# Raw statistics held behind the table's last part, all third parts copied by VectorE, and the bias's parts spread by one product, in a graph layer's kernel

## The chip, the cores and the metric

The kernel runs on one core of a Trainium2 chip. The metric is the device time of one execution in microseconds (us); the time before is the median of three runs. The engines are called PE (TensorE, matrix products), ACT (ScalarE), DVE (VectorE), POOL (GpSimd) and SP (SyncE, which here only issues DMAs). PEld is TensorE's weight load. "L504" is line 504 of the kernel before.

## What is computed

A graph layer with 12,500 nodes of 128 features, 200,000 edges and 4 edge types. Edges are sorted by their target node; sources and types are random, and the targets crowd toward low node numbers. Cut to what matters:

```python
h = jnp.maximum(_layernorm(x, axis=-1), 0.0)          # x: 12500 x 128, fp32
xs = h[src]                                            # 200000 rows
msgs = 0
for i in range(4):                                     # W: 4 x 128 x 128, b: 4 x 128
    msgs = msgs + jnp.where((edge_type == i)[:, None], xs @ W[i] + b[i], 0.0)
out = x + jax.ops.segment_sum(msgs, dst, num_segments=12500)
```

## The kernel before

The kernel sums source rows per target node and type first and multiplies by W afterwards. Edges come in chunks of 128. A one-hot matrix of a chunk (edge by target and type) turns the sum into a TensorE product. The lowest target nodes have so many edges that they go another way: edges are counted per node, type and source, and the counts are multiplied with the whole of h. It has three stages, which overlap.

**The table and the slots (0 to about 119 us).** h is written to DRAM as a table (`htab`), each fp32 number as three bf16 parts whose sum is that number. The nodes are cut into 33 spans of up to three rows for each of the 128 partitions. For each span:

- `load_span` loads x by SP (L190 to L192) into one of 11 buffers (`hm`).
- `look` gives five steps as functions: the statistics of each row (`bn_stats`, DVE, L440), their sums (DVE, L444 to L449), the root (ACT, L452), the scales (DVE, L455 and L456) and the normalisation with relu (ACT, L461).
- `first_part` normalises and copies h to the first bf16 part (ACT, L487), and PE puts h minus that part into PSUM (L490 and L491).
- `second_part` copies that difference to the second part (ACT, L496), and PE subtracts it too (L497).
- `third_part` copies what is left to the third part: for odd spans by ACT (L502), for even ones by DVE (L504). Then SP writes the span's three parts to `htab` (L506). The difference lies in one of four PSUM banks in turn (two named `ps`, one `py`, one `pa`), and the three parts in one of five buffers `h3`.

The parts of neighbouring spans are taken in turn: first part of span u, second part of u − 1, third part of u − 2. Between them the code also issues steps of `ring_rows`, a generator that prepares small things. Among these are the bias's three bf16 parts, as `b12` (12 rows: part c of type t in row 4c + t) and as `b128` (128 rows: part c of type t in row 32t + c, all other rows zero). It zeroes `b128` (DVE, L1180), then copies the 12 rows one by one with 12 DMAs of SP (L1196, 256 bytes each). `b128` is first used by the main loop's weighting (`weigh`, L605), `b12` by the slots and the raw groups.

The slots are the work list of the dense part. `make_slots` finds for each of the lowest nodes where its edges lie: DVE one-hots (L816) times edge data on PE (L825, L854, L857), unpacking and comparing on DVE (L837 to L842, L866 to L871, L883 to L897, L913 to L918), a product that counts edges by type (PE, L903), its copy with a running sum (ACT, L904), the bias's share of these nodes (PE, L925) and its copy (ACT, L933). One-hots, products and copies of the 512-column pieces are pipelined by generators; their PSUM tiles are the four `pt` banks.

**The raw groups (to about 157 us).** The first 48 chunks don't wait for the table. Their rows of x are gathered by GpSimd (`gather_raw`, L528) while the table is made. Then `add_up_raw` treats them in three groups of 16: statistics (L440, tile `str`), sums, root, scales, normalisation in place (L461, tile `hx`), one-hots (DVE, L620), and fp32 products (PE, L635, L641, L646, L648) with copies by ACT (L636, L643). The normalisations of raw rows are also marks that the first gathers of the main loop from `htab` (POOL, L544) are tied to.

**The main loop (to 1649 us).** All other chunks in groups of 16: gathers from `htab` (L544), one-hots (L561), products (L578), copies (L581), weighting (L596 to L605), and adding into a ring of node sums (L666). The dense part runs beside it: one-hots (L957, L965), counts (L983, L989) and the products of counts with h (L1033), for which SP loads `htab` back in order (L1029).

The program is written in one order, and a scheduler that works from the program's dependences orders each engine's instructions before the run. An engine then works strictly in its order. The function `held_by` adds a dependence by hand, which both orders two instructions and makes the second wait for the first.

Of the kernel before, what the change touches and what calls it, by code (L numbers as in the profile page):

```python
# [35 lines left out]
F32 = mybir.dt.float32  # L36
BF16 = mybir.dt.bfloat16
# [11 lines left out]
P = 128  # L49
# [25 lines left out]
def kernel(  # L75
# [10 lines left out]
    nc = tc.nc  # L86
    N, D = x.shape
    E = src.shape[0]
    NT, _, DO = w.shape
# [7 lines left out]
    N3 = 3 * NT  # L97
# [10 lines left out]
    q = E0 / E  # L108
# [37 lines left out]
    for i, n in enumerate(sizes_of):  # L146
# [4 lines left out]
        of = alone[3 * many_at : 3 * (many_at + n1)]  # L151
# [269 lines left out]
    CG = P // NT  # L421
# [10 lines left out]
    def look(xt, n, tag, wide):  # L432

        sums2 = aheads.tile([P, wide, 2], F32, name="mv" + tag)
        var = aheads.tile([P, wide], F32, name="var" + tag)
        rstd = aheads.tile([P, wide], F32, name="rstd" + tag)
        nmr = aheads.tile([P, wide], F32, name="nmr" + tag)
        st = aheads.tile([P, wide, 2, 3], F32, name="st" + tag)
        looks = [
            lambda k=k: nc.vector.bn_stats(st[:, k].rearrange("p h s -> p (h s)"), xt(k)).ins for k in range(n)  # L440
        ]

        def spread():
            nc.vector.tensor_tensor(sums2[:, :n], st[:, :n, 0, 1:], st[:, :n, 1, 1:], ALU.add)  # L444
            nc.vector.tensor_tensor(var[:, :n], st[:, :n, 0, 1], st[:, :n, 1, 1], ALU.subtract)
            nc.vector.scalar_tensor_tensor(
                var[:, :n], var[:, :n], 0.25 * D, var[:, :n], op0=ALU.mult, op1=ALU.mult
            )
            nc.vector.tensor_tensor(var[:, :n], var[:, :n], sums2[:, :n, 1], ALU.add)  # L449

        def root():
            nc.scalar.activation(rstd[:, :n], var[:, :n], AF.Sqrt, bias=eps, scale=1.0 / D)  # L452

        def scales():
            nc.vector.reciprocal(rstd[:, :n], rstd[:, :n])  # L455
            nc.vector.scalar_tensor_tensor(  # L456
                nmr[:, :n], sums2[:, :n, 0], -0.5, rstd[:, :n], op0=ALU.mult, op1=ALU.mult
            )

        def normalize(k, h):  # L460
            return nc.scalar.activation(  # L461
                h, xt(k), AF.Relu, bias=nmr[:, k : k + 1], scale=rstd[:, k : k + 1]
            ).ins

        return looks, spread, root, scales, normalize
# [11 lines left out]

    banks = [(s_ps, "ps"), (s_ps, "ps"), (y_ps, "py"), (a_ps, "pa")]
    splits = {}

    def first_part(u, one):
        n = spans[u][1] - spans[u][0]
# [15 lines left out]

    def third_part(u):
        ps, h3, n = splits.pop(u)  # L500
        if u % 2:
            nc.scalar.copy(h3[:, :n, 2, :], ps)  # L502
        else:
            nc.vector.tensor_copy(h3[:, :n, 2, :], ps)  # L504
        j0, j1 = spans[u]
        nc.sync.dma_start(  # L506
            htab.rearrange("(p j) f -> p j f", j=NW)[:, j0:j1, :], h3[:, :n].rearrange("p j c d -> p j (c d)")
        )
# [8 lines left out]
    def held_by(one, by, reason):  # L517
        tc.add_manual_dep(
            one.ins,
            by.name,  # L520
            mybir.DependencyInfo(mybir.DependencyClass.Sync, mybir.DependencyReason.DATA),
            reason=reason,
        )
# [86 lines left out]
    def add_up_raw(t0, g, rows, marked):  # L610
        win = window_of(C0 + t0)
        K = NT * win
        row = lambda k: rows(k)
        looks, spread, root, scales, normalize = look(row, g, "r", G)
        for l in looks:
            l()
        spread()
        root()
        oh = rawp.tile([P, G, KR], F32, name="ohf", bufs=2)[:, :, :K]
        nc.vector.tensor_tensor(  # L620
            oh,
            iota_f[:, :K].unsqueeze(1).to_broadcast([P, g, K]),
            keyf[:, t0 : t0 + g].unsqueeze(2).to_broadcast([P, g, K]),
            ALU.is_equal,
        )
        yield True
        scales()
        done = [normalize(k, row(k)) for k in range(g)]
        marked.extend(done[4::5])
        yield True  # L630
        sb = spool.tile([P, G * KM], F32, name="sb")[:, : G * K].rearrange("p (g t n) -> p g t n", g=G, t=NT)
        for i0 in range(0, g, SG):
            ps = s_ps.tile([P, 512], F32, name="ps")[:, : SG * K].rearrange("p (i n) -> p i n", i=SG)
            for i in range(i0, i0 + SG):
                nc.tensor.matmul(ps[:, i - i0, :], rows(i), oh[:, i, :], start=True, stop=True)  # L635
            nc.scalar.copy(sb[:, i0 : i0 + SG].rearrange("p g t n -> p g (t n)"), ps)  # L636
            yield True
        ohv = oh.rearrange("p g (t n) -> p g t n", t=NT)
        pc = s_ps.tile([P, 512], F32, name="ps")[:N3, : G * win].rearrange("p (g n) -> p g n", g=G)
        for t in range(NT):  # L640
            nc.tensor.matmul(pc, pick_f[:, t, :], ohv[:, :, t, :], start=(t == 0), stop=(t == NT - 1))  # L641
        cnt = spool.tile([N3, G * WIN], BF16, name="cnt")[:, : G * win].rearrange("p (g n) -> p g n", g=G)
        nc.scalar.copy(cnt, pc)  # L643
        yield True
        py = raw_py[:, t0 * win : (t0 + g) * win].rearrange("p (g n) -> p g n", g=G)
        nc.tensor.matmul(py, b12, cnt, start=True, stop=False)  # L646
        for t in range(NT):
            nc.tensor.matmul(py, wsb[:, t, :], sb[:, :, t, :], start=False, stop=(t == NT - 1))  # L648
        yield True
# [521 lines left out]
    def ring_rows():  # L1171
        nc.vector.tensor_single_scalar(over, heads, RING.bit_length() - 1, op=ALU.arith_shift_right)
        nc.vector.scalar_tensor_tensor(heads, over, -float(RING), heads, op0=ALU.mult, op1=ALU.add)
        nc.vector.tensor_scalar(heads, heads, 0.0, float(RING - 1), ALU.max, ALU.min)
        nc.sync.dma_start(heads_d, heads)
        nc.sync.dma_start(brow, heads_d.rearrange("(o q) c -> o (q c)", o=1))
        yield True
        part12 = prep.tile([N3, 3], F32, name="part12")
        nc.vector.tensor_reduce(part12, ident[:N3, :N3].rearrange("p (c t) -> p c t", c=3), AX.X, ALU.add)
        nc.vector.memset(b128, 0.0)  # L1180
        bs = prep.tile([N3, DO], F32, name="bs")
        for c in range(3):
            bh = prep.tile([N3, DO], BF16, name="bh")
            nc.vector.tensor_copy(bh, bf)
            if c == 0:
                nc.vector.tensor_scalar(bs, bh, part12[:, 0:1], None, ALU.mult)
            else:
                nc.vector.scalar_tensor_tensor(bs, bh, part12[:, c : c + 1], bs, op0=ALU.mult, op1=ALU.add)
            if c < 2:
                nc.vector.tensor_sub(bf, bf, bh)  # L1190
            yield True
        nc.vector.tensor_copy(b12, bs)
        for t in range(NT):
            for c in range(3):
                k = c * NT + t
                nc.sync.dma_start(b128[t * CG + c : t * CG + c + 1, :], b12[k : k + 1, :])  # L1196
        yield True

    group_of = []
# [20 lines left out]
    for gi, us in enumerate(group_of):  # L1220
        here, at_here = ahead, at
        more_looks = []
        if gi + 1 < len(group_of):
            for u in group_of[gi + 1]:
                while len(queue) <= u:
                    queue.append(load_span(len(queue)))
            ahead, at = look_at(group_of[gi + 1])
            more_looks = list(ahead[0])
        each = -(-len(more_looks) // max(1, len(us) - 1))
        for i, u in enumerate(us):  # L1230
            while len(queue) < min(NU, u + 14):
                queue.append(load_span(len(queue)))
            first_part(u, lambda k, h: here[4](at_here[u, k], h))
            if u:
                second_part(u - 1)
            if u > 1:
                third_part(u - 2)
            last = None
            for l in more_looks[:each]:
                last = l()  # L1240
            del more_looks[:each]
            while last is not None and len(raws) < min(NRAW, 3 + (u + 1) * NRAW // (NU - 4)):
                raws.append(gather_raw(len(raws), last))
            if gi + 1 < len(group_of):
                if i == max(0, len(us) - 2):
                    ahead[1]()
                    ahead[2]()
                if i == len(us) - 1:
                    ahead[3]()
            if u >= 3:  # L1250
                next(small, None)
# [270 lines left out]
```

## Time and profile before

| | us |
|---|---|
| median of three runs | 1648.86 (1646.37 to 1652.16) |
| profiled execution, its own time | 1651.06 |
| profiled execution, span of the trace | 1649.2 |
| PE busy in the span | 1457.4 (88%) |
| DVE busy | 1041.5 (63%) |
| POOL busy | 1011.6 (61%) |
| ACT busy | 458.7 (28%) |

The span runs from the first to the last instruction; the execution's own time has 1.86 us more around it. A group of instructions is shown as: line, engine, operation, out<-in, (partitions x elements, type), count | busy us, mean ns of one | idle time of that engine just before them, and what ended it. A row of a timeline is: start, length, engine, line, operation, out<-in, count, and in brackets the idle time before it and what released it; "issue" means that the engine waited for nothing that the profile shows. Records of neighbouring instructions can overlap by some tenths of a microsecond. A queue row (SPq) is the time in which SP issues a DMA, not the transfer.

### The profile page before, as it was taken

The numbers are of one execution on the slowest core, as the hardware profiler recorded it, in microseconds if no ns is written. First come the engines' busy times: TensorE is split into PE (matmuls) and PEld (weight loads), VectorE is DVE, ScalarE is ACT, GpSimd is POOL, SyncE is SP. The second block draws the span as 40 slices with busy tenths as digits, with TensorE's granted clock in tenths as the row PEclk, the third lists the DMA queues.
The fourth block names the chain that finished last, engine by engine and source line by source line (L and its number), as shares of the span: only waits on it lengthen the run. The fifth ranks groups of instructions, "written<-read, shape, count | busy, mean of one in ns | idle before, by whom it ended". The sixth has DMA issues, their size and how long they took to land.

```text
span 1649.2 us, 33169 instructions
## 1 busy us (share of the span) xinstructions
PE 1457.4 (88%) x11293; PEld 958.5 (58%) x11293; DVE 1041.5 (63%) x5387; ACT 458.7 (28%) x1121; POOL 1011.6 (61%) x1062
## 2 busy tenths in 40 slices
PE   5678789999899999999999999999999999998975
PEld 2236476666566566666666666656565656565654
DVE  8792977666585766657576666657564756574333
ACT  6494222222222222222222222222222222222011
POOL 7435566666666666666666666666666566666562
PEclk9785799999999999999999999999999999999997
DMA  7452377766667766666666667666666566666652
GB/s 221 129 212 75 107 220 220 217 197 213 200 206 211 217 194 212 197 208 208 207 202 201 200 209 220 181 210 203 180 219 198 175 194 211 184 189 193 210 169 70
DMA packets 138411, 317.02 MB, mean 192 GB/s; under 512 B 25880, under 2 KB 78666, under 8 KB 138235
## 3 DMA queue, kind: packets, MB, share of 16 engines
q1 hardware_dynamic: 89323, 214.61, 41.7%
q0 software_dynamic: 48912, 100.24, 20.8%
q8 instruction: 89, 1.46, 0.4%
q14 instruction: 87, 0.71, 0.1%
HBM read 298.71 MB, written 16.04 MB: 191 GB/s over the span
## 4 chain that ended last, share of the span: by engine, by line
PE 81%; issue 8%; DVE 8%; ACT 2%; DMA 1%; DVEq 0%; SPq 0%; POOL 0%; ACTq 0%
PE pa L1033 47%; PE pt L983 12%; PE py L605 7%; PE ps L578 7%; DVE o L957 1%; PE pt L1047 1%; PE ps L635 1%; PE py L596 1%; PE pt L691 1%; DVE oh L561 1%; DVE o L965 1%; DVE ring L666 1%; PE pt L857 1%; DVE stt L440 1%; PE pt L854 0%
## 5 line engine op out<-in xcount | busy, mean ns | idle before, releaser
L544 POOL DMA_INDIRECT hm<-htab,srcT x987 | 954.7, 967 | 575.6 <-issue 226.0
L1033 PE MATMUL pa<-counts,hs 128*128 128x324 fp8e4 (+1 forms) x5586 | 1000.5, 304 | 50.2 <-issue 47.1
L1033 PEld LDWEIGHTS <-hs 128*128 128x128 bf16 x5586 | 519.0, 96 | 325.1 <-issue 84.7
L957 DVE TENSOR_SCALAR o<-iota_n,hkT 128x392 bf16<-128x392 f16 x1211 | 401.2, 331 | 75.4 <-PE pt L983 30.6
L983 PE MATMUL pt<-o,o 128*128 128x396 bf16 x1211 | 378.4, 336 | 37.0 <-DVE o L965 20.0
L989 ACT CAST counts<-pt 128x396 int32<-128x396 f32 x506 | 242.1, 493 | 500.5 <-PE pt L983 172.1
L561 DVE TENSOR_SCALAR oh<-iota_b,keyT 128x56 bf16<-128x56 bf16 (+8 forms) x987 | 167.7, 261 | 265.6 <-PE ps L578 94.6
L581 ACT COPY sb<-ps 128x224 f32<-128x224 f32 (+8 forms) x247 | 98.4, 399 | 480.3 <-PE pt L983 165.0
L578 PE MATMUL ps<-oh,hm 128*128 128x56 bf16 (+8 forms) x2961 | 189.1, 198 | 38.0 <-issue 35.3
L578 PEld LDWEIGHTS <-hm 128*128 128x128 bf16 x2961 | 163.0, 99 | 96.5 <-issue 49.1
L666 DVE TENSOR_TENSOR ring<-ring,py 128x14 f32 (+7 forms) x960 | 167.7, 175 | 65.0 <-PE pa L1033 13.0
L965 DVE TENSOR_SCALAR o<-iota,loT 128x128 bf16<-128x128 bf16 x660 | 178.4, 270 | 0.0
L983 PEld LDWEIGHTS <-o 128*128 128x128 bf16 x1211 | 114.8, 97 | 96.2 <-DVE o L965 27.4
L965 DVE TENSOR_SCALAR o<-iota,loT,byT 128x128 bf16<-128x128 bf16 x461 | 155.4, 337 | 0.0
L605 PE MATMUL py<-sb,wsb 128*128 128x224 f32 (+7 forms) x480 | 129.5, 412 | 1.3 <-issue 1.0
L605 PEld LDWEIGHTS py<-sb,wsb 128*128 128x128 f32 x480 | 88.2, 196 | 27.6 <-issue 5.6
L997 DVE COPY bi<-counts 128x27 int32<-128x27 int32 (+1 forms) x19 | 4.2, 220 | 113.3 <-issue 64.7
L528 POOL DMA_INDIRECT hx<-in_x_dram,srcT x48 | 51.3, 1069 | 35.9 <-DVE stt L440 22.4
L600 ACT CAST cnt<-py 128x224 bf16<-128x224 f32 (+7 forms) x60 | 23.7, 396 | 93.3 <-PE ps L578 29.9
L461 ACT ACTIVATE h<-hm,nmrt,rstdt 128x128 f32<-128x128 f32 x98 | 43.0, 493 | 1.0 <-DVE mvt L444 0.5
L1047 PE MATMUL pt<-sd,wsb 128*128 128x81 f32 (+1 forms) x152 | 25.8, 325 | 4.6 <-issue 4.6
L490 PE MATMUL ps<-h,ident 128*128 128x384 f32 (+1 forms) x34 | 16.3, 563 | 12.7 <-issue 11.6
(235 smaller groups left out, 666.6 us busy)
## 6 DMA issues: line engine op xcount, KB each, us to landing
hs<-htab SPq DMA_DIRECT2D x304, 576.0 KB
hm<-htab,srcT POOLq DMA_INDIRECT x987
htab<-h SPq DMA_DIRECT2D x32, 288.0 KB
xo<-in_x_dram SPq DMA_DIRECT2D x24, 256.0 KB
out_dram<-xo SPq DMA_DIRECT2D x24, 256.0 KB
hs<-htab SPq DMA_DIRECT2D x19, 192.0 KB
hm<-in_x_dram SPq DMA_DIRECT2D x18, 192.0 KB
hm<-in_x_dram SPq DMA_DIRECT2D x14, 168.0 KB
```

The source lines that it names most:

```text
L528: one = nc.gpsimd.indirect_dma_start(out=hm[:, i * D : (i + 1) * D], out_offset=None, in_=x, in_offset=bass.IndirectOffsetOnAxis(ap=srcf[: ...
L544: one = nc.gpsimd.indirect_dma_start(out=hm[:, (i - h0) * D3 : (i - h0 + 1) * D3], out_offset=None, in_=htab, in_offset=bass.IndirectOffse ...
L561: nc.vector.tensor_scalar(oh[:, i, :], iota_b[:, :K], keyf[:, at : at + 1], None, ALU.is_equal)
L578: nc.tensor.matmul(ps[:, i - i0, :], rows(i, c), oh[:, i, :], start=(c == 0), stop=(c == 2))
L581: nc.scalar.copy(sb[:, i0:i1].rearrange("p g t n -> p g (t n)"), ps[:, : i1 - i0, :])
L605: nc.tensor.matmul(py[:, :g, :], wsb[:, t, :], sb[:, :g, t, :], start=False, stop=(t == NT - 1))
L666: nc.vector.tensor_tensor(to, to, of(i), ALU.add)
L957: one = nc.vector.tensor_scalar(o2[:, k, :NB], iota_n, hkT[:, s : s + 1], None, ALU.is_equal)
L965: one = nc.vector.tensor_scalar(o1[:, k], iota_1, loT[:, s : s + 1], by, ALU.is_equal, ALU.mult)
L983: one = nc.tensor.matmul(pb, o1, o2, start=first, stop=last)
L989: nc.scalar.copy(counts[:, :, i * NT : (i + 1) * NT], pb.rearrange("p (b t) -> p b t", t=NT))
L1033: nc.tensor.matmul(pa[:, : 3 * nu * NT].rearrange("p (m v) -> p m v", m=3), hs[:, j - j0, c * D : (c + 1) * D], of, start=(j == 0 and c == 0),
```

## The change

Four edits:

1. `third_part` always copies by VectorE, and keeps each copy instruction in the list `thirds`.
2. `look`'s statistics functions return the instruction's handle (callers take `.ins` where they need it), and in `add_up_raw` the first statistics instruction of the second and third group (t0 is 16 or 32) is held by the last entry of `thirds`, which is the copy of the table's last third part.
3. `b128` is no longer zeroed and filled by 12 DMAs. A 12 x 128 bf16 matrix `spread12` with a one at (4c + t, 32t + c) is made from the identity (GpSimd memset, one DVE copy); PE multiplies it with `b12` into a `pt` bank, and DVE copies the bank to `b128`. The product's entries are single bf16 values, so `b128` is the same.
4. `look_at`'s loop takes `.ins` of what `look` returns, without any other effect.

```diff
--- before.py
+++ after.py
@@ -437,7 +437,7 @@
         nmr = aheads.tile([P, wide], F32, name="nmr" + tag)
         st = aheads.tile([P, wide, 2, 3], F32, name="st" + tag)
         looks = [
-            lambda k=k: nc.vector.bn_stats(st[:, k].rearrange("p h s -> p (h s)"), xt(k)).ins for k in range(n)
+            lambda k=k: nc.vector.bn_stats(st[:, k].rearrange("p h s -> p (h s)"), xt(k)) for k in range(n)
         ]
 
         def spread():
@@ -477,6 +477,7 @@
 
     banks = [(s_ps, "ps"), (s_ps, "ps"), (y_ps, "py"), (a_ps, "pa")]
     splits = {}
+    thirds = []
 
     def first_part(u, one):
         n = spans[u][1] - spans[u][0]
@@ -498,10 +499,7 @@
 
     def third_part(u):
         ps, h3, n = splits.pop(u)
-        if u % 2:
-            nc.scalar.copy(h3[:, :n, 2, :], ps)
-        else:
-            nc.vector.tensor_copy(h3[:, :n, 2, :], ps)
+        thirds.append(nc.vector.tensor_copy(h3[:, :n, 2, :], ps).ins)
         j0, j1 = spans[u]
         nc.sync.dma_start(
             htab.rearrange("(p j) f -> p j f", j=NW)[:, j0:j1, :], h3[:, :n].rearrange("p j c d -> p j (c d)")
@@ -612,8 +610,10 @@
         K = NT * win
         row = lambda k: rows(k)
         looks, spread, root, scales, normalize = look(row, g, "r", G)
-        for l in looks:
-            l()
+        for k, l in enumerate(looks):
+            one = l()
+            if t0 and not k:
+                held_by(one, thirds[-1], "rows of x are looked at behind the table")
         spread()
         root()
         oh = rawp.tile([P, G, KR], F32, name="ohf", bufs=2)[:, :, :K]
@@ -1177,7 +1177,6 @@
         yield True
         part12 = prep.tile([N3, 3], F32, name="part12")
         nc.vector.tensor_reduce(part12, ident[:N3, :N3].rearrange("p (c t) -> p c t", c=3), AX.X, ALU.add)
-        nc.vector.memset(b128, 0.0)
         bs = prep.tile([N3, DO], F32, name="bs")
         for c in range(3):
             bh = prep.tile([N3, DO], BF16, name="bh")
@@ -1190,10 +1189,14 @@
                 nc.vector.tensor_sub(bf, bf, bh)
             yield True
         nc.vector.tensor_copy(b12, bs)
-        for t in range(NT):
-            for c in range(3):
-                k = c * NT + t
-                nc.sync.dma_start(b128[t * CG + c : t * CG + c + 1, :], b12[k : k + 1, :])
+        spread12 = prep.tile([N3, P], BF16, name="spread12", bufs=1)
+        nc.gpsimd.memset(spread12, 0.0)
+        nc.vector.tensor_copy(
+            spread12.rearrange("k (t q) -> k t q", q=CG)[:, :, :3], ident[:N3, :N3].rearrange("k (c t) -> k t c", t=NT)
+        )
+        pb = x_ps.tile([P, DO], F32, name="pt")
+        nc.tensor.matmul(pb, spread12, b12, start=True, stop=True)
+        nc.vector.tensor_copy(b128, pb)
         yield True
 
     group_of = []
@@ -1237,7 +1240,7 @@
                 third_part(u - 2)
             last = None
             for l in more_looks[:each]:
-                last = l()
+                last = l().ins
             del more_looks[:each]
             while last is not None and len(raws) < min(NRAW, 3 + (u + 1) * NRAW // (NU - 4)):
                 raws.append(gather_raw(len(raws), last))
```

## The prediction

> **What bounds the kernel now.** I read the page first, then the span cut into stages, then the timeline of each engine at the two places that the diff touches. The page gives the length, and who makes the chain that ended last.
>
> ```profile
> span 1649.2 us, 33169 instructions
> ...
> PE 81%; issue 8%; DVE 8%; ACT 2%; DMA 1%; DVEq 0%; SPq 0%; POOL 0%; ACTq 0%
> ```
>
> TensorE sets the end, but that is the mean over a main loop which the diff leaves alone. The cut into stages shows where the edited code runs: columns are the stretch, then busy us and instructions of each engine, the granted TensorE clock, the DMA share and GB/s.
>
> ```profile
> core 0: us, PE busy (x) PEld busy (x) DVE busy (x) ACT busy (x) POOL busy (x), PEclk, DMA share, GB/s
> ...
> 20.00:46.65 26.65, 19.84 (x60) 7.86 (x60) 25.77 (x110) 24.53 (x63) 21.16 (x19) 0.94 0.80 250
> 46.65:60.00 13.35, 2.77 (x5) 0.89 (x5) 3.45 (x19) 2.84 (x8) 7.58 (x9) 0.59 0.28 82
> 60.00:118.80 58.80, 51.01 (x218) 22.81 (x217) 55.43 (x209) 46.32 (x120) 15.73 (x15) 0.91 0.49 164
> 118.80:154.50 35.70, 32.73 (x143) 27.89 (x143) 8.80 (x45) 21.27 (x61) 19.86 (x21) 0.50 0.34 112
> ...
> 192.00:1649.00 1457.00, 1325.20 (x10726) 886.49 (x10724) 900.97 (x4728) 344.40 (x823) 911.87 (x943) 0.98 0.65 198
> ```
>
> From 20 to 118.8 us, while the table and the slots are made, VectorE is busy 25.77 of 26.65 and 55.43 of 58.80 us, so it is the bound there, with TensorE close behind in the second stretch (51.01). In between lies a hole of 13.35 us in which VectorE works 3.45, ScalarE 2.84 and TensorE 2.77: **9.90 us of VectorE idle**. The SyncE, VectorE, ScalarE and TensorE timelines there:
>
> ```profile
> 46.56 0.69 SPq L506 DMA_DIRECT2D htab<-h  x1
> 48.15 11.68 SPq L1196 DMA_DIRECT2D b<-b  x12
> ...
> 54.72 0.71 SPq L1196 DMA_DIRECT2D b<-b  x1
> ...
> 56.18 0.70 SPq L1196 DMA_DIRECT2D b<-b  x1
> ...
> 59.86 0.33 SPq L190 DMA_DIRECT2D hm<-in_x_dram  x1
> ```
> ```profile
> 48.20 1.00 DVE L839 TENSOR_TENSOR nth<-nth,qa 128x1480 f16<-128x1480 f16 x1 [1.54 <-issue]
> ...
> 53.28 0.56 DVE L504 CAST h<-ps 128x384 bf16<-128x384 f32 x1 [3.72 <-PE ps L497]
> ...
> 54.74 0.16 DVE L842 TENSOR_SCALAR qa<-qa 128x1 f16<-128x1 f16 x1 [0.31 <-issue]
> ...
> 56.20 0.16 DVE L842 TENSOR_SCALAR qa<-qa 128x1 f16<-128x1 f16 x1 [1.30 <-issue]
> ...
> 60.04 1.40 DVE L816 TENSOR_SCALAR sel<-qa,cidx 128x512 f16<-128x512 f16 x5
> ```
> ```profile
> 59.88 0.48 ACT L496 CAST h<-ps 128x384 bf16<-128x384 f32 x1 [6.60 <-remote]
> ...
> 60.44 0.59 PE L854 MATMUL pt<-sel,what 128*128 128x512 f16 x1 [6.07 <-DVE sel L816]
> ```
>
> The hole spans the twelve issues of L1196, the bias rows. VectorE's tiny instructions start 0.05, 0.02 and 0.02 us behind issues (48.15/48.20, 54.72/54.74, 56.18/56.20), and ScalarE and VectorE are free at 59.88 and 60.04, as the next queue entry (59.86) starts. I read that as: these twelve issues hold the other engines up. Why, no row says.
>
> **The end of this stage.** Normalising raw group 1 (hx, L461) on ScalarE opens the raw stage, and TensorE then sets its end, 32.73 of 35.70 us busy. The VectorE and ScalarE timelines just before:
>
> ```profile
> 106.29 0.22 DVE L896 TENSOR_SCALAR sel<-hkT 128x136 bf16<-128x136 f32 x1
> ...
> 106.98 0.55 DVE L504 CAST h<-ps 128x384 bf16<-128x384 f32 x1
> ...
> 108.63 0.81 DVE L620 TENSOR_TENSOR ohf<-iota_f,keyT 128x640 f32<-128x640 f32 x1
> ...
> 110.03 0.16 DVE L449 TENSOR_TENSOR varr<-varr,mvr 128x16 f32<-128x16 f32 x1
> ...
> 111.08 0.54 DVE L504 CAST h<-py 128x384 bf16<-128x384 f32 x1
> ...
> 114.01 0.41 DVE L504 CAST h<-ps 128x256 bf16<-128x256 f32 x1
> ```
> ```profile
> 114.42 0.26 ACT L904 ACTIVATE d<-pt 12x136 bf16<-12x136 f32 x1
> 114.58 0.18 ACT L904 ACTIVATION_READ_ACCUMULATOR d<-pt 12x1 f32 x1
> ...
> 116.64 0.52 ACT L452 ACTIVATE rstdr<-varr,eps 128x16 f32<-128x16 f32 x2
> ...
> 117.50 6.27 ACT L461 ACTIVATE hx<-hx,nmrr,rstdr 128x128 f32<-128x128 f32 x16 [0.35 <-DVE nmrr L456]
> ```
>
> Group 1's sums were ready at 110.19, yet its root (L452) runs at 116.64: in ScalarE's order it stands behind L904 (114.76) and L933, which come late because the slots' last one-hots, done at 106.51, wait in ScalarE's and TensorE's order behind the table.
>
> **The change part by part.** The sum follows the start of that first raw normalise, 117.50 us.
>
> *The bias product.* The twelve issues go, and the hole with them: −9.90 us for VectorE if I read it rightly, nothing if the cause lies elsewhere. In their place come a memset on GpSimd, a product of 12 rows, and two small VectorE copies less one memset; I take +0.3 us, from 0.16 (one tiny instruction above) to 1.0 (two 0.5-us copies).
>
> *Third parts on VectorE.* Spans are 33; sixteen odd ones move over.
>
> ```profile
> L502 ACT CAST h<-ps 128x384 bf16<-128x384 f32 x8 | 3.8, 478 | 0.8 <-PE ps L497 0.8
> ...
> L504 DVE CAST h<-py 128x384 bf16<-128x384 f32 x8 | 4.4, 550 | 1.4 <-issue 0.6 <-PE pt L903 0.5 <-PE py L497 0.2
> ...
> 78.43 0.54 DVE L504 CAST h<-ps 128x384 bf16<-128x384 f32 x1
> 78.89 0.25 DVE L455 RECIPROCAL rstdt<-rstdt 128x18 f32<-128x18 f32 x1
> ```
>
> Records overlap: the instruction behind a copy starts 78.89 − 78.43 = 0.46 us later. So 16 × 0.46 = **+7.4 us** on VectorE, the bound (16 × 0.55 = 8.8 at most). ScalarE is relieved of 16 instructions of 478 ns (at most 7.6 us), worth nothing by itself, since it is busy 46.32 of 58.80 us; without that cover nothing would be lost either. Queued behind each moved copy are the slot steps, and TensorE's pick-outs wait for these.
>
> *The order.* The built order puts all 33 third parts ahead of the last slot one-hots, so three that ran behind them (106.98, 111.08, 114.01) now run before: 0.46 + 0.46 + 0.34 = +1.3 us. In exchange L904 and L933 no longer have table work in front of them on ScalarE.
>
> *The hold.* The first statistics of raw groups 2 and 3 wait for the last third part. In the built order both stand behind that part on VectorE anyway, so the wait adds nothing (what it may have done to the order is in the terms above); were it binding, what is queued behind it is 32 statistics, which group 2's normalise needs only when 16 others (6.27 us) are through. No DMA moves with it, and the table's writes come earlier on SP.
>
> *The sum.* Last one-hots ready: 106.51 − 9.90 + 7.4 + 1.3 + 0.3 = 105.6. Behind them one 12-row product (0.4, my estimate) and L904 (0.34 from start to end: 114.42 to 114.76) give 106.4. From there to the root took 116.64 − 114.76 = 1.88 through L933; VectorE has about as much left for group 1's sums (a compare of 0.81, and by the built order four statistics and four sums: some 2.4, an estimate), so 108.8; root to normalise 0.86: **109.7, or 7.8 us earlier**. Against this stands TensorE: it must now do the same products in some ten us less, and was already 87% busy (51.01 of 58.80), so VectorE's in-order copies will wait for L497. The waits seen are 0.2 us in eight copies above; the ceiling is the 3.4 us that VectorE idled in that stretch, once again. I take +2, between 0.4 (16 copies at that rate) and 3.4: **−5.8**.
>
> The raw stage (37 us) and the main loop (1457 us) shift without change, since the first table gathers of L544 are tied to that root and the main loop's order is the same. Profiled 1651.06 us (span 1649.2, 1.9 around it) becomes 1645.3; the profiled execution lay 2.2 above the median 1648.86, so by the median **1643 us**.
>
> *The clock.* The granted clock is 0.59 in the hole and 0.91 behind it; when TensorE has work again, its first 512-column product takes 0.59 us. The Trainium skill ("TensorE: Matmul & The Clock Gate", Part 1, What's actually happening) says that the array falls to half clock after an idle window of about 3.4 us and comes back after as long a busy one. The hole agrees with it; by it the raw stage, 92% busy, should be warm, where the trace grants 0.50, so I don't count on it.
>
> **The rivals.**
>
> A, the forecast: −4 to −9 us, 1640 to 1645. For it: the starts within 0.02 us of the issues.
>
> B, the gain is eaten: TensorE takes over as the bound. It has 51.01 us of products in that stretch; at the 94% at which VectorE was fed (55.43/58.80) they need 54, so the stretch could shrink by no more than 4.5, less what the hole's own 2.77 and the copies' waits take. Net −4 to +2, some 1648. For it: 87%. Against: part of those products ran at half clock.
>
> C, slower: the hole stays, filled by something else on SP's queue, for instance the twelve were only the next in line behind the table's reads and writes. Then the 9.90 don't come back while 7.4 to 8.8 of copies do: −5.8 + 9.9 = +4.1, and with the upper copies and waits +6.9: 1653 to 1656. The point: it turns slower once 5.8 of the 9.9 stay. Against it: DMA share in the hole is 0.28, so nothing is saturated.
>
> D, more: with no hole TensorE stays warm, and the raw stage runs at full clock. ScalarE then bounds it: 48 normalises at 6.27/16 = 0.39 are 18.8, and it was 21.27 busy, against 35.70 now: up to −14 more, down to 1632. The table stretch alone could give 2. Against: the clock stayed 0.50 through 33 us of steady products.
>
> E, the change does not do what it says: the hold binds nothing, for the statistics it names stood late before too, behind group 1's, whose sums end at 110.19. I hold that likely, 0.8; it goes with any of the four and shifts none, at 0 us.
>
> **How the numbers follow.** A 0.50, B 0.20, C 0.18, D 0.12. About 0.3% (5 us, the line at 1643.9) is what a measurement of this kernel can tell from no change. Of A, 0.36 lies below that line and 0.14 above. Faster: 0.36 + 0.12 = 0.48; same: 0.14 + 0.20 = 0.34; slower: 0.18. A's own range is 1640 to 1645. The range reaches to 1637, into D, and to 1654, into C's middle.
>
> **What would show it.** Right: no L1196 rows; VectorE busy from 46 to 60 us; 33 third parts under one VectorE line; raw hx at 109 to 113; first main products (L578) near 148, 154.08 before:
>
> ```profile
> 154.08 0.38 PE L578 MATMUL ps<-oh,hm 128*128 128x40 bf16 x6
> ```
>
> Wrong: a hole of the same length around other issues (C); VectorE's copies waiting for L497 by more than 5 us in all (B); a clock above 0.6 in the raw stage (D); or a main loop that isn't 1495 us from that product to the end, which would put the cause where no step of mine looks.

## The result, and the profile after

| | before | after |
|---|---|---|
| median of 22 runs each, same chip, us | 1648.91 (1644.0 to 1654.63) | 1655.78 (1648.62 to 1661.58) |
| ratio | | 1.0038, 95% interval 1.0028 to 1.0048 |
| span of the profiled execution, us | 1649.2 | 1651.7 |
| VectorE idle from 20 to 60 us | 10.79 | 10.53 |
| slots' last one-hots end, us | 106.51 | 116.55 |
| first raw normalisation starts, us | 117.50 | 121.30 |
| first product of the main loop (L578 before, L576 after), us | 154.08 | 157.09 |

The changed kernel is slower by 6.9 us, where 6 us less was forecast. The forecast was wrong in sign.

The page of the changed kernel, its length and the makers of the chain that ended last, and the cut into the prediction's stages (columns as there):

```profile
span 1651.7 us, 33178 instructions
...
PE 80%; issue 9%; DVE 8%; ACT 2%; DMA 1%; another core or an unknown queue 1%; DVEq 0%; SPq 0%; POOL 0%; ACTq 0%
```
```profile
core 0: us, PE busy (x) PEld busy (x) DVE busy (x) ACT busy (x) POOL busy (x), PEclk, DMA share, GB/s
...
20.00:46.65 26.65, 16.61 (x38) 6.19 (x39) 18.27 (x70) 18.74 (x49) 16.19 (x17) 0.71 0.63 204
46.65:60.00 13.35, 10.94 (x30) 3.51 (x28) 11.20 (x45) 7.30 (x19) 8.93 (x10) 0.81 0.56 180
60.00:118.80 58.80, 48.32 (x214) 22.19 (x213) 54.76 (x193) 39.76 (x101) 19.30 (x17) 0.89 0.46 159
118.80:154.50 35.70, 30.38 (x131) 27.07 (x130) 17.91 (x93) 23.79 (x66) 18.36 (x19) 0.50 0.35 115
```

The old hole is filled: from 46.65 to 60 us VectorE works 11.20 us, where it was 3.45. But the stretch ahead of it has lost as much: 18.27 of 26.65, where it was 25.77. Together VectorE idles 26.65 − 18.27 + 13.35 − 11.20 = 10.53 us, against 0.88 + 9.90 = 10.78 before (10.79 by the cut from 20 to 60 us at once). **The hole wasn't removed; it moved forward.** The timelines of VectorE, ScalarE, TensorE, SyncE and GpSimd at its new place:

```profile
34.21 0.56 DVE L502 CAST h<-py 128x384 bf16<-128x384 f32 x1 [2.37 <-PE ps L491]
...
38.40 0.34 DVE L1187 SCALAR_TENSOR_TENSOR bs<-bh,part,bs 12x128 f32<-12x128 bf16 x1 [1.81 <-remote]
41.23 0.56 DVE L502 CAST h<-pa 128x384 bf16<-128x384 f32 x1 [2.48 <-PE ps L491]
```
```profile
36.30 0.48 ACT L497 CAST h<-pa 128x384 bf16<-128x384 f32 x1 [4.16 <-issue]
...
41.26 0.48 ACT L497 CAST h<-ps 128x384 bf16<-128x384 f32 x1 [2.91 <-PE ps L491]
```
```profile
36.84 0.48 PE L498 MATMUL pa<-h,minus 128*128 128x384 bf16 x1 [3.73 <-issue]
```
```profile
34.84 0.70 SPq L190 DMA_DIRECT2D hm<-in_x_dram  x1
35.56 0.69 SPq L191 DMA_DIRECT2D hm<-in_x_dram  x1
36.94 0.70 SPq L192 DMA_DIRECT2D hm<-in_x_dram  x1
...
41.18 0.29 SPq L190 DMA_DIRECT2D hm<-in_x_dram  x1
```
```profile
36.54 0.94 POOL L526 DMA_INDIRECT hx<-in_x_dram,srcT  x1 [0.47 <-issue]
37.79 0.94 POOL L526 DMA_INDIRECT hx<-in_x_dram,srcT  x1 [0.30 <-issue]
44.17 0.95 POOL L526 DMA_INDIRECT hx<-in_x_dram,srcT  x1 [5.43 <-DVE b L1191]
```

The picture is that of before: VectorE, ScalarE, TensorE and SyncE stand idle for microseconds at a time, start again together (VectorE and ScalarE at 41.23 and 41.26, behind SyncE at 41.18), and SyncE's issues take 0.70 us. Only this time SyncE issues plain row loads (L190 to L192), which take 0.29 us as soon as the hole is over. The twelve bias issues are gone, and can't be the cause. GpSimd gathers raw rows back to back until 38.73 us, and the hole ends 2.5 us after that. In the kernel before, GpSimd's timeline has the last gather of such a row here:

```profile
55.73 0.94 POOL L528 DMA_INDIRECT hx<-in_x_dram,srcT  x1 [0.31 <-issue]
```

It ended at 56.67, and the hole at 59.86.

The end of the stage, on VectorE and ScalarE, and the main loop's first product:

```profile
105.58 0.42 DVE L502 CAST h<-ps 128x256 bf16<-128x256 f32 x1
...
116.33 0.22 DVE L896 TENSOR_SCALAR sel<-hkT 128x136 bf16<-128x136 f32 x1
```
```profile
117.50 0.27 ACT L904 ACTIVATE d<-pt 12x136 bf16<-12x136 f32 x1 [2.03 <-PE pt L903]
...
120.34 0.31 ACT L452 ACTIVATE rstdr<-varr,eps 128x16 f32<-128x16 f32 x1 [0.30 <-DVE varr L449]
121.30 6.26 ACT L461 ACTIVATE hx<-hx,nmrr,rstdr 128x128 f32<-128x128 f32 x16 [0.65 <-DVE nmrr L456]
```
```profile
157.09 0.38 PE L576 MATMUL ps<-oh,hm 128*128 128x40 bf16 x6
```

The table's last third part is done at 106.0, 8.4 us earlier than before, and the slots' last one-hots 10.0 us later. From them to the normalisation it takes 4.75 us, where it took 10.99, because ScalarE and TensorE have no table work left and now wait for VectorE (2.03 us before that L904). So 10.04 − 6.24 = 3.80 us remain.

### The profile page after: what moved, and what is told of

Same layout as the page of the kernel before. It is cut to its first block, busy times and chain, and to the rows that moved or that the text cites. A ratio compares the mean times of both kernels' runs of the same rounds, so it can differ in the third digit from the quotient of the medians.

```text
span 1651.7 us, 33178 instructions
## 1 busy us (share of the span) xinstructions
PE 1460.8 (88%) x11294; PEld 959.7 (58%) x11294; DVE 1046.6 (63%) x5404; ACT 453.4 (27%) x1105; POOL 1015.0 (61%) x1063
## 4 chain that ended last, share of the span: by engine, by line
PE 80%; issue 9%; DVE 8%; ACT 2%; DMA 1%; another core or an unknown queue 1%; DVEq 0%; SPq 0%; POOL 0%; ACTq 0%
PE pa L1033 46%; PE pt L983 12%; PE py L603 7%; PE ps L576 7%; DVE o L957 1%; PE pt L1047 1%; DVE ring L666 1%; DVE oh L559 1%; PE ps L635 1%; PE pt L691 1%; PE py L594 1%; DVE o L965 1%; ACT h L461 1%; PE ps L491 1%
## 5 line engine op out<-in xcount | busy, mean ns | idle before, releaser
L576 PE MATMUL ps<-oh,hm 128*128 128x56 bf16 (+8 forms) x2961 | 189.9, 197 | 44.6 <-issue 40.4
L576 PEld LDWEIGHTS <-hm 128*128 128x128 bf16 x2961 | 163.3, 98 | 106.9 <-issue 62.8
L526 POOL DMA_INDIRECT hx<-in_x_dram,srcT x48 | 46.0, 958 | 34.7 <-DVE stt L440 13.7
```

Source lines behind the costliest of these rows:

```text
L576: nc.tensor.matmul(ps[:, i - i0, :], rows(i, c), oh[:, i, :], start=(c == 0), stop=(c == 2))
```

## The experiments

Two theories. **Theory 1** is the prediction's: the twelve issues hold the other engines up. **Theory 2**: the hole has another cause, and falls on whatever SyncE issues at the time; the suspect is GpSimd's raw gathers. Four of the runs (the bias product alone, the copies alone, the changed kernel without the hold, and the raw gathers spread in pairs) and before shared one chip; the others ran on two further ones, where before takes 1672 to 1674 us. Ratios are against before on the same chip. Rows of a timeline or a cut come from one profiled execution of each kernel.

**The bias product alone.** Before, with the 12 DMAs and the memset replaced by the changed kernel's product:

```diff
-        nc.vector.memset(b128, 0.0)
...
-        for t in range(NT):
-            for c in range(3):
-                k = c * NT + t
-                nc.sync.dma_start(b128[t * CG + c : t * CG + c + 1, :], b12[k : k + 1, :])
+        spread12 = prep.tile([N3, P], BF16, name="spread12", bufs=1)
...
+        nc.tensor.matmul(pb, spread12, b12, start=True, stop=True)
+        nc.vector.tensor_copy(b128, pb)
```

> Before with the bias product alone: the twelve DMAs of L1196 and the memset go, third parts stay alternating, nothing is held. Theory 1 (that of the prediction: these twelve issues hold the other engines up): the idle of VectorE between 20 and 60 us, 10.8 us in the kernel before (0.88 + 9.90), falls below 4 us, the raw normalisation starts 7 to 10 us earlier than 117.5, and the ratio is 0.994 to 0.996. Theory 2 (the hole has another cause and only fell on these issues): VectorE's idle from 20 to 60 us stays between 8 and 13 us, at another place, and the ratio lies within 0.998 to 1.002.

Measured: 1648.29 us, ratio 0.9994 (0.9981 to 1.0006). The cut from 20 to 60 us shows VectorE idle for 9.54 us:

```profile
20.00:60.00 40.00, 24.94 (x69) 9.46 (x67) 30.46 (x136) 27.83 (x71) 27.15 (x27) 0.79 0.64 201
```

Removing the issues is worth nothing that can be measured in the time. In its one profile the raw normalisation did start 4.0 us earlier, at 113.50, though the slots' last one-hots ended later (109.42): here too the table's last third part is done before them, at 106.22. The main loop's first product came 4.8 us earlier (149.29), and yet the span was only 1.0 us shorter, for the main loop took 1498.9 us from there, where it took 1495.1. Why isn't known; an earlier start of the raw stage need not be an earlier end.

**All third parts on VectorE, alone.** The bias DMAs stay:

```diff
-        if u % 2:
-            nc.scalar.copy(h3[:, :n, 2, :], ps)
-        else:
-            nc.vector.tensor_copy(h3[:, :n, 2, :], ps)
+        nc.vector.tensor_copy(h3[:, :n, 2, :], ps)
```

> Before with all third parts copied by VectorE and nothing else; the twelve DMAs stay. Both theories: 16 copies more on VectorE at 0.46 us, so that the slots' last one-hots (106.5 us before) end 7 to 10 us later and the ratio is 1.003 to 1.006. Theory 1: the hole of some 10 us stays on the issues of L1196. Theory 2: it lies wherever else, of like length. If the copies are not what made the changed kernel slower, the ratio is below 1.002.

Measured: 1655.56 us, ratio 1.0042 (1.0025 to 1.0059): the whole loss of the changed kernel. The slots' last one-hots end at 115.42 us, 8.9 us later than before. The hole lies at 31 to 41 us, in front of the twelve issues, which come at 55.08 here. The timelines of VectorE and SyncE in this kernel:

```profile
40.85 0.56 DVE L501 CAST h<-pa 128x384 bf16<-128x384 f32 x1 [4.55 <-remote]
```
```profile
55.08 7.05 SPq L1193 DMA_DIRECT2D b<-b  x12
```

The twelve take 7.05 us here, where they took 11.68, and VectorE waited at most 1.97 us beside them (for a product). The copies alone make the loss of the changed kernel, as far as the two intervals can tell.

**The changed kernel without the hold.**

```diff
-        for k, l in enumerate(looks):
-            one = l()
-            if t0 and not k:
-                held_by(one, thirds[-1], "rows of x are looked at behind the table")
+        for l in looks:
+            l()
```

> The changed kernel without the hold on the raw statistics. VectorE's built order is the same, so both theories expect the changed kernel's time: ratio to before 1.002 to 1.006, and the raw normalisation at 121 us within 2 us. If the hold costs anything by itself, this is faster than the changed kernel by more than 0.2%.

Measured: 1652.23 us, ratio 1.0018 (1.0005 to 1.0030), raw normalisation at 121.24 where it was 121.30. The profile is that of the changed kernel, but the interval barely meets the changed kernel's (1.0028 to 1.0048), so it may be that the hold costs 0.2%. The next run takes it by itself.

**The hold alone**, with third parts alternating (the list `thirds` holds ScalarE's and VectorE's copies) and the bias DMAs:

```diff
+        copy = nc.scalar.copy if u % 2 else nc.vector.tensor_copy
+        thirds.append(copy(h3[:, :n, 2, :], ps).ins)
...
+            if t0 and not k:
+                held_by(one, thirds[-1], "rows of x are looked at behind the table")
```

> Before with the hold alone (first statistics of the second and third raw group behind the table's last third part); third parts alternate and the twelve DMAs stay. VectorE's built order is that of the kernel before, where the held instruction stood at 109.83 us or later and the last third part ended at 114.4. If the hold is nothing: ratio 0.999 to 1.001. If it costs by itself (the changed kernel without it measured 1.0018, with it 1.0038): above 1.0015, with the statistics of the later groups starting behind 114.4 us and the raw products of these groups later by some us.

Measured: 1673.30 us, ratio 1.0004 (0.9991 to 1.0017). The hold by itself is nothing that can be measured, so it doesn't explain the 0.2% above. The three kernels with all third parts on VectorE measured 1.0042 (copies alone), 1.0038 (the whole change) and 1.0018 (without the hold); their intervals meet between 1.0028 and 1.0030. That the copies cost is shown; whether the hold or the bias product moves their cost by 0.2% is not.

**Raw gathers spread over the table.** Before, with each pair of gathers held by a third part instead of by statistics that run far ahead:

```diff
+        thirds.append(copy(h3[:, :n, 2, :], ps).ins)
...
-            last = None
             for l in more_looks[:each]:
-                last = l()
+                l()
             del more_looks[:each]
-            while last is not None and len(raws) < min(NRAW, 3 + (u + 1) * NRAW // (NU - 4)):
-                raws.append(gather_raw(len(raws), last))
+            while u > 1 and len(raws) < min(NRAW, 3 + (u - 1) * NRAW // (NU - 4)):
+                raws.append(gather_raw(len(raws), thirds[-1]))
```

> Before, with GpSimd's raw gathers tied to the copies of third parts, so that they come spread over the table instead of one behind the other from 18 to 57 us; all else stays, the twelve DMAs too. Theory 1: the hole on the issues of L1196 stays (VectorE idle from 20 to 60 us 8 to 13 us), ratio 0.999 to 1.001. Theory 2 in the form that the hole comes from gathers running back to back beside SyncE's transfers (in both traces it ends within 3 us of a pause of the gathers): VectorE's idle from 20 to 60 us falls below 6 us and the ratio is 0.993 to 0.998.

Measured: 1643.38 us, ratio 0.9958 (0.9943 to 0.9973), with the twelve issues in place. The cut from 20 to 60 us:

```profile
20.00:60.00 40.00, 30.27 (x90) 12.53 (x90) 35.52 (x153) 31.29 (x79) 22.66 (x23) 0.83 0.62 191
```

VectorE's idle falls to 4.48 us, the raw normalisation starts at 109.31, the main loop's first product at 146.04. Theory 1 falls, theory 2 holds. **This version beats both kernels.**

**No raw gathers.** Before, with GpSimd clearing the tiles instead, from the fourth on, so that the rows of 42 of the first 48 chunks are left out of the sums:

```diff
+            if k < 3:
+                one = nc.gpsimd.indirect_dma_start(
...
+            else:
+                one = nc.gpsimd.memset(hm[:, i * D : (i + 1) * D], 0.0)
```

> Before, where all raw gathers but the first three tiles' are replaced by a memset of their tile on GpSimd: the rows of x for 42 of the first 48 chunks are left out of the sums. The twelve DMAs, SyncE's loads and table writes and the third parts stay. If the hole comes from the gathers beside SyncE's transfers, VectorE's idle from 20 to 60 us (10.8 us before, 4.5 with the gathers spread) falls below 3 us, and SyncE's single issues of about 0.7 us go away in that stretch but for those of L1196. If it comes from SyncE's transfers or from the sheer pace of instructions, an idle of 6 us or more stays, perhaps elsewhere.

Measured, in a single execution, which gives no time to compare: VectorE idles 1.26 us from 20 to 60 us. The row of SyncE's issues and of VectorE's one-column instructions (L842 before, L845 here), which in the kernel before came one for each issue, 0.7 to 1.5 us apart:

```profile
43.95 8.14 SPq L1199 DMA_DIRECT2D b<-b  x12
```
```profile
46.18 0.56 DVE L845 TENSOR_SCALAR qa<-qa 128x1 f16<-128x1 f16 x8
```

Eight of them now run in 0.56 us, in the middle of the same twelve issues. That is the cleanest test of the prediction's reading: same instructions, same issues, no gathers but the first few, no hole.

**Late raw gathers.** Before, with the gathers held to third parts from span 14 on:

```diff
...
+            while u > 14 and len(raws) < min(NRAW, 3 + (u - 14) * NRAW // (NU - 17)):
+                raws.append(gather_raw(len(raws), thirds[-1]))
```

> Before, with the raw gathers from the fourth on tied to third parts from span 14 on, so that none runs between about 20 and 60 us and they come close together after that. If gathers back to back beside SyncE's loads make the hole: VectorE idles below 3 us from 20 to 60 us, and more than in the kernel before (3.4 us) from 60 us to the raw normalisation; ratio 0.993 to 1.000. If the hole belongs to the stretch and not to the gathers, 8 us or more of idle stay between 20 and 60 us, ratio 1.000 to 1.005.

Measured: 1684.45 us, ratio 1.0082 (1.0066 to 1.0097). The cut from 20 to 60 and to 118.8 us, of this kernel and then of the one without gathers:

```profile
20.00:60.00 40.00, 32.52 (x115) 13.77 (x115) 39.41 (x167) 32.09 (x81) 6.43 (x6) 0.96 0.58 186
60.00:118.80 58.80, 41.77 (x146) 16.94 (x144) 40.09 (x138) 36.72 (x91) 35.40 (x35) 0.79 0.46 149
```
```profile
20.00:60.00 40.00, 31.07 (x114) 13.28 (x114) 38.74 (x166) 30.97 (x80) 5.51 (x22) 0.96 0.54 176
```

Third of the engine columns: VectorE idles 0.59 us in the first stretch, and 18.71 in the second, into which the gathers were moved (GpSimd busy 35.40 us there, 15.73 before). The hole follows the gathers. Its longest stretch ends 2.3 us behind a row of 14 gathers (62.04 to 80.31; VectorE starts again at 82.60). But gathers one behind the other don't always make one: from 94 to 107 us, with gathers all along, VectorE works 11.74 of 13 us. The forecast of the ratio was a miss: crowded, they cost more than where they were.

**Single raw gathers, evenly.** As the spread pairs, but each gather is held by itself: one for each span up to the middle of the table, two after it.

```diff
+            while u > 1 and seen_raw < min(NRAW * HG, 3 * HG + (u - 1) + max(0, u - 17)):
+                k, part = divmod(seen_raw, HG)
+                hm = gather_raw(k, thirds[-1], [part])
...
```

> Before with single raw gathers tied to third parts, one for each span up to the middle of the table and two for each span after it, so that GpSimd pauses between them. If the hole comes from gathers that run back to back for ten us or longer: VectorE's idle from 20 to 60 us, 10.8 us before and 4.5 with pairs tied to spans, falls below 3 us, and the ratio to below 0.996. If the number of gathers in the stretch counts and not their spacing, the idle stays at 3 to 5 us and the ratio at 0.995 to 0.997.

Measured: 1669.85 us, ratio 0.9981 (0.9970 to 0.9991). The idle from 20 to 60 us falls to 1.38 us, about as low as without gathers, with 15 gathers in that stretch (15.96 us of GpSimd), where the pairs put 23. So fewer gathers, further apart, leave no hole there; the number and the spacing aren't told apart. But the ratio is worse than with pairs, a miss. Two for each span then run mostly back to back from 65 to 103 us (VectorE idles 6.3 of these 38 us), and VectorE has a wait again just before the raw stage, in its timeline:

```profile
104.59 0.56 DVE L503 CAST h<-py 128x384 bf16<-128x384 f32 x1 [4.56 <-PE pa L492]
```

**The bias product with spread gathers.** Both edits as above, together, on before.

```diff
...
-                nc.sync.dma_start(b128[t * CG + c : t * CG + c + 1, :], b12[k : k + 1, :])
...
+        nc.tensor.matmul(pb, spread12, b12, start=True, stop=True)
...
-            while last is not None and len(raws) < min(NRAW, 3 + (u + 1) * NRAW // (NU - 4)):
-                raws.append(gather_raw(len(raws), last))
+            while u > 1 and len(raws) < min(NRAW, 3 + (u - 1) * NRAW // (NU - 4)):
+                raws.append(gather_raw(len(raws), thirds[-1]))
```

> Before, with the bias product and with the raw gathers spread; third parts alternate, nothing is held. If the twelve issues cost nothing by themselves, this equals the spread gathers alone (0.9958): ratio 0.994 to 0.9975. If they cost what the prediction took for them, or a part, now that the gathers don't stand in the way, it is below 0.993.

Measured: 1665.89 us, ratio 0.9967 (0.9955 to 0.9980), VectorE's idle 6.16 us. Not below the spread gathers alone (0.9958): no cost of the twelve issues shows here either.

**The changed kernel with spread gathers.** Against the changed kernel:

```diff
...
-            while last is not None and len(raws) < min(NRAW, 3 + (u + 1) * NRAW // (NU - 4)):
-                raws.append(gather_raw(len(raws), last))
+            while u > 1 and len(raws) < min(NRAW, 3 + (u - 1) * NRAW // (NU - 4)):
+                raws.append(gather_raw(len(raws), thirds[-1]))
```

> The changed kernel with the raw gathers spread in the same way. If the hole and the copies add up: VectorE's idle from 20 to 60 us falls from 10.5 us to below 6, and the ratio to before is 0.996 to 1.001 (changed kernel 1.0038, less the 0.42% that spreading was worth to the kernel before). If VectorE's copies are bad only because they crowd the table ahead of the slots while gathers run, it is below 0.995.

Measured: 1675.20 us, ratio 1.0020 (1.0009 to 1.0031), a little outside what was expected. The idle falls only to 7.27 us, so the gain is some half of what it was for the kernel before.

**All third parts on ScalarE, with spread gathers**: the opposite of the change.

```diff
+        copy = nc.scalar.copy
+        thirds.append(copy(h3[:, :n, 2, :], ps).ins)
```

> Before with the raw gathers spread in pairs, and all 33 third parts copied by ScalarE: the opposite of the change's move. If VectorE's copies lie on the path that sets the raw stage's start (0.46 us each), 17 fewer on VectorE bring the raw normalisation 3 to 8 us earlier than the 109.3 us of the spread gathers alone, ratio 0.991 to 0.995. If ScalarE becomes the bound instead (it was busy 49.5 of 58.8 us there and gets 6.3 us more), the ratio is 0.996 to 1.000.

Measured: 1674.66 us, ratio 0.9998 (0.9981 to 1.0014). The slots' last one-hots end at 97.97 us, but the raw normalisation starts only at 116.09: now the table on ScalarE is what comes last: its last copy ends at 112.11 us, and L903, L932 and the root follow it without a wait of more than 0.33 us. With third parts alternating (on the first chip) the same two were 98.53 and 109.31. In these orders neither engine can take all copies without coming last.

**Eleven of the sixteen copies.** Before, with ScalarE's copies kept up to span 10:

```diff
-        if u % 2:
+        if u % 2 and u < 11:
```

> Before, with the odd third parts copied by VectorE only from span 11 on: 11 of the 16 copies move, the first five stay on ScalarE, and by the built order the slots' first one-hots stand after four third parts, as in the kernel before, and not after eleven as in the changed kernel. If the copies cost by their own work on VectorE, some 11/16 of what all of them cost (1.0042): ratio 1.002 to 1.004, with the slots' last one-hots about 5 to 6 us later than 106.5 us. If they cost because the first ones push the slots' start back (34.6 us before, 48 to 49 with all copies moved), the ratio is 0.999 to 1.001.

Measured: 1673.79 us, ratio 1.0003 (0.9987 to 1.0019). VectorE's and ScalarE's timelines of this kernel:

```profile
111.99 0.22 DVE L896 TENSOR_SCALAR sel<-hkT 128x136 bf16<-128x136 f32 x1
```
```profile
117.61 6.29 ACT L461 ACTIVATE hx<-hx,nmrr,rstdr 128x128 f32<-128x128 f32 x16 [0.65 <-DVE nmrr L456]
```

The time is what was expected if the copies cost by pushing the slots' start back; the one-hots' end is what was expected if they cost by their own work. They end 5.7 us later (11 × 0.46 = 5.1), and yet the raw normalisation starts where it did in the kernel before, 117.50. The rows show how: it comes 5.40 us behind the one-hots here (112.21 to 117.61), 4.75 in the changed kernel, and 10.99 in the kernel before. So the first 6 us or so by which VectorE comes later are covered by what ScalarE's and TensorE's order took behind the one-hots before, and of all sixteen copies the part beyond that cover shows. This reading was made after the run. The earlier start of the slots, which this kernel also has (38.05 us against 49.45 in the changed kernel), isn't told apart from it.

## Why the prediction was wrong, point by point

**The step that failed** is "these twelve issues hold the other engines up". The starts of VectorE's instructions within 0.02 to 0.05 us of the issues were taken as cause and effect (the first of the three, L839, isn't a tiny instruction, but one of 1.00 us). With no issue of L1196 at all the hole stays (10.53 us in the changed kernel, 9.54 with the bias product alone), and it goes with the gathers. GpSimd stood in the very row of the stage that showed the hole (7.58 us busy, more than any other engine), and the prediction shows no row of its timeline there. The term was −9.90 us, and measured −0.26. With −0.26 in its place the prediction's own sum gives 121.3 us for the raw normalisation, and 121.30 was measured. That it is so close is partly luck: VectorE's added work was 1.1 us more than forecast and the way behind the one-hots 0.65 us longer, while the 2 us of waits didn't come.

**The copies** were sized nearly right. The cut up to the end of the last one-hots, of before and then of after:

```profile
0.00:20.00 20.00, 5.11 (x10) 2.06 (x11) 15.52 (x118) 7.80 (x20) 13.59 (x36) 1.00 0.66 187
20.00:60.00 40.00, 22.61 (x65) 8.75 (x65) 29.21 (x128) 27.36 (x70) 28.74 (x27) 0.82 0.63 194
60.00:106.51 46.51, 44.19 (x179) 19.33 (x178) 43.34 (x150) 34.87 (x87) 14.58 (x13) 0.93 0.48 160
```
```profile
0.00:20.00 20.00, 5.00 (x10) 1.95 (x11) 15.60 (x117) 7.68 (x20) 13.78 (x37) 1.00 0.65 186
20.00:60.00 40.00, 27.55 (x67) 9.70 (x67) 29.47 (x113) 26.04 (x67) 25.12 (x27) 0.74 0.61 196
60.00:116.55 56.55, 46.07 (x194) 21.17 (x193) 53.10 (x186) 38.81 (x98) 19.30 (x17) 0.91 0.47 163
```

VectorE was busy 15.52 + 29.21 + 43.34 = 88.07 us before and 15.60 + 29.47 + 53.10 = 98.17 after: 10.10 more, where 7.4 + 1.3 + 0.3 = 9.0 were forecast. By kind, these are nineteen copies of third parts (the sixteen, and the three that ran behind the one-hots before), one raw statistic, and two small copies for the bias in place of the memset. The table's groups of copies in the changed kernel show the mean times that were assumed, 0.55 us each:

```profile
L502 DVE CAST h<-ps 128x384 bf16<-128x384 f32 (+1 forms) x17 | 9.2, 544 | 4.6 <-PE ps L498 3.6 <-issue 1.0
L502 DVE CAST h<-py 128x384 bf16<-128x384 f32 x8 | 4.4, 551 | 2.8 <-PE ps L491 2.4 <-PE py L498 0.4
L502 DVE CAST h<-pa 128x384 bf16<-128x384 f32 x8 | 4.4, 551 | 4.3 <-PE ps L491 2.5 <-PE pa L498 1.7
```

**The copies' waits** for TensorE (+2, up to 3.4) did not show as a term of their own: all VectorE idle up to that point is 18.38 us, before 18.44.

**The order behind the one-hots** held: 4.1 us from them to the normalisation were forecast (105.6 to 109.7), 4.75 measured, 10.99 before. What shortens it is that the table ends before the last one-hots, and not ScalarE's relief, which is worth nothing by itself, as forecast: with the bias product alone, where ScalarE keeps its copies, it was 4.08. The prediction's sum had this saving, and it hides the first 6 us of the copies.

**The hold** by itself is nothing, as forecast (rival E's condition), and **the bias product** by itself is nothing in time.

**The raw stage and the main loop** shifted without change in the profiles: from the first main product to the end 1495.1 us before and 1494.6 after, the raw stage's clock 0.50 in both. So D fell, as did A. B fell too: there was no gain for TensorE to eat, and its busy time from 60 to 118.8 us went down, from 51.01 to 48.32.

**Rival C** named the right size (1653 to 1656) and the right form, a hole that stays and falls on something else. Its cause, something else on SyncE's queue, isn't what the runs show: without the gathers the same queue entries make no hole.

What stays open: the profiles show 3.0 us at the main loop's first product and 2.5 us in the span, the medians 6.9. The profiled execution of before lay 2.2 us above its median and that of after 2.4 us below its own, so one profile each can't say where the rest lies.

## What to carry to other kernels

When several engines stop together and start together, look at the one that doesn't stop: the instruction that starts with them, or that the hole ends on, may be slowed as they are. A hole is only removed if the total idle of the stretch falls; compare sums over a stretch that holds both the old and the new place. And before an engine's work is moved to another, measure how much later the receiver may be before it becomes the last one: here about 6 us, by the rows behind the one-hots, where 10 were added.

## What the runs showed of the hardware

While GpSimd gathered rows by indirect DMA, 0.94 us each with 0.30 between, one behind the other beside the table's work, VectorE, ScalarE, TensorE and SyncE stood idle for up to 6.6 us at a time (ScalarE in the kernel before), and SyncE's issues took 0.70 us instead of 0.3. Instructions also started long after what they read was there. In the kernel before, ScalarE's L496 at 59.88 us reads this product, which had ended at 54.37:

```profile
53.85 0.52 PE L491 MATMUL ps<-h,minus 128*128 128x384 bf16 x1
```

VectorE's idle from 20 to 60 us was 9.5 to 11.5 us in every kernel with the gathers as before (with or without the twelve DMAs, the copies or the hold), 4.5 to 7.3 with pairs spread, 1.4 with single gathers spread, 1.3 with memsets in their place, and 0.6 with only six gathers, at the stretch's end (50.50 to 58.45 us).

Gathers in a row are not enough for a hole. In the kernel before they run from 18.48 us on without a pause, and VectorE idles only 0.88 us from 20 to 46.65; the hole comes in the last ten us of this row of 28, which ends at 56.67, and 3.2 us beyond. In the changed kernel it comes in the last seven of a row of 16 (18.59 to 38.73), and 2.5 us beyond. What has to come together, and which part of a gather does it, is open. The DMA engines were not full: the DMA share in the hole before was 0.28. The Trainium skill ("SBUF — State Buffer", Who interferes with whom) says that only the port pair which VectorE and GpSimd share makes engines wait for each other, and that TensorE and ScalarE never wait for it. That alone doesn't explain a hole that stops ScalarE, TensorE and SyncE as well.
